# Two layers on graphs: the first pairs of phase A start closer together, and a broadcast add becomes a bias

## The chip, the cores and the metric

The kernel runs on one core of a Trainium2 chip. The metric is the device time of one execution in microseconds; of several executions the median counts. The core has five engines with a queue each: TensorE (PE in the profile) for matrix products, VectorE (DVE), ScalarE (ACT) and GpSimd (POOL) for elementwise work, and SyncE (SP), which here issues all DMAs. They run side by side and wait for each other by semaphores. Each works off its own queue in order.

## The reference

128 graphs of 64 nodes with 768 features, all in float32. Layer 0 is a graph attention with 12 heads of 64, followed by a gate, a residual and a layer norm. Layer 1 is a masked attention with 6 heads of 128, followed by the same.

```python
# layer 0
h = einsum('bnd,ade->bane', x, W);  th = tanh(h)
attn = einsum(th, w_src) + swapaxes(einsum(th, w_dst), 2, 3)   # src of the row + dst of the column
attn = where(attn >= 0, attn, 0.2 * attn)
attn = softmax(where(~adj[:, None], -999.0, attn))
f = elu(einsum('banm,bame->bane', attn, h) + b)
gate = sigmoid(x @ H_w.T + H_b)
x = layernorm(x + gate * f + (1 - gate) * x)
# layer 1
q, k, v = x @ Wq + bq, x @ Wk + bk, x @ Wv + bv
probs = softmax(q k^T / sqrt(128) + where(adj, 0, -9e15))
x = layernorm(x + (probs v) @ Wf + bf)
```

## The kernel before

The 8192 rows (graph, node) are 64 tiles of 128 rows, that is, two graphs each. Two tiles make a pair; there are NP = 32 pairs. Phase A does layer 0 and the v of layer 1, pair by pair. Phase B does the rest of layer 1 and isn't touched.

**Products.** A pair's dense product (W for h, G for the gate, V for layer 1's v) is done in the manner of Strassen, by seven blocks instead of eight. `Product.matmuls` (L217) issues block i as three matmuls of 128 x 384 (L208), which stand in the trace as six. Blocks 0, 2, 4 and 6 add into one PSUM bank X; block 1 has Z, blocks 3 and 5 have Y. Between them the partial sums must be taken out: after blocks 0, 2 and 3 ScalarE copies the bank to a `snap` (L404), after blocks 1, 4 and 5 VectorE adds bank and snap into the result (L427, L446), and after block 6 ScalarE copies it (L425, L444). So block 2 waits for the snap of block 0, block 4 for that of block 2, and block 5 for that of block 3. The left operands are the transposed rows T and four sums S of them, made by GpSimd (`token_sums`, L254).

**Transposed rows.** VectorE turns blocks of 32 x 32 (`turn`, L383), and the DMAs `load_blocks` (L370, four issues a tile) set the blocks into place. Layer 1's v needs the output of layer 0 in this form: it is spilled to DRAM (`spill`, L621), loaded as blocks (`x1_in`), turned and stored (`x1T`), and summed (`x1_sums`).

**Steps.** The order is written out by hand. `at(step, f)` puts a function on a list, and `run` (L262) calls the lists step by step; what is called emits instructions in that order, for each engine's queue. Within a step the order is that of the calls of `at`: earlier pairs come first. A step is one block of a dense product. Pair p starts at o = N * p with N = 21: W in steps o to o+6, G in o+7 to o+13, and in o+14 to o+20 the V of the pair two before it (v = o + 56, L736). Three pairs are moved by hand: V of pair NP-4 (28) goes to the end (o + 84), with its T loaded again from DRAM (`reload_T`); NP-2 and NP-1 have 50 and 45. So steps 14 to 20 of pairs 0, 1 and NP-2 (30) hold no V.

**The chain of a tile.** The rest of a pair is a chain for each tile, `Tile0`; tile 1 starts at s = o, tile 0 at s = o + 5 (L678). With s as zero: tanh of h on ScalarE (6; tile 0 one later), products with w_dst and w_src on GpSimd (7, 8), their sums on VectorE (9, 10), `dst_out` to DRAM and `exchange` of half of h between partitions by DMA (9), `dst_in` back as a broadcast over the rows (12 or 13), `add` (17): GpSimd adds `src` as a broadcast (L515), ScalarE applies the leaky activation (Prelu, L518); `mask` and `top` on VectorE (18), `exp` head by head on ScalarE (19, 20; L531), `scale` on GpSimd (21, 22; L541), `probs` and `aggregate` on TensorE (24, 25; L552, L570), `elu`, `mix1`, `mix2`, `norm1`, `norm2`, `spill` (26 to 31). Where `z` is three less (tile 1 of pairs 0, 1 and NP-2) add, mask, exp and scale come three steps earlier. `gate_in` (GpSimd, L580) and `gate` (ScalarE, L584) come at o+14 to o+18.

**Places.** `xb` has seven places of a tile. x and the adjacency of a pair are loaded together at o - 20 (`load`, L319) into place (2p + i) % 7. h and the gate (`gt`) have three buffers each, T four, S two, s two, hx two. The blocks of x are asked for at o - 20 and o - 16 and turned at o - 6 and o - 5, earlier by `lead` in pairs 1, 2 and NP-1.

Of the kernel before, what the change touches and what calls it, by code (L numbers as in the profile page):

```python
# [61 lines left out]
def kernel(  # L62
# [31 lines left out]
    nc = tc.nc  # L94
    NB, S, D = x.shape
    A, _, E = W.shape
    HEADS = 6
    DH = D // HEADS
    NC = D // P
# [3 lines left out]
    NP = NT // 2  # L103
# [201 lines left out]
    def phase_a(ctx):  # L305
# [6 lines left out]
        st = [dict() for _ in range(NP)]  # L312
        sds = []
        for i in range(2):
            sd = k1.tile([P, 32], F32, name=f"sd{i}")
            nc.vector.memset(sd, 0.0)
            sds.append(sd)

        def load(p):  # L319
            d = st[p]  # L320
            d["x"] = []
            for i in range(2):
                t = xb[:, (2 * p + i) % 7]
                nc.sync.dma_start(t, x_t[2 * p + i])
                d["x"].append(t)
            d["adj"] = small.tile([P, 2, S], U8, name="adj")
            nc.sync.dma_start(d["adj"], adj_p[p])

        load(0)

        w0 = weight_tile(0)
        w0_v = w0.rearrange("p s c o -> p s (c o)").rearrange(
# [10 lines left out]

        def load_hrow(oc):

            name = ("gt", "gt", "gt", "z", "tmp", "th")[oc]
            hrows[oc] = k3.tile([P, D], F32, name=name, bufs=3 if oc < 3 else 1)
            nc.sync.dma_start(hrows[oc], H_w[oc * P : (oc + 1) * P, :])

        def hw_blocks(oc):  # L350
# [56 lines left out]
        def sums(d):  # L407
            Ss = k6.tile([P, 4, CH, P], F32, name="S")
            token_sums(Ss, *d["T"])
            d["S"] = Ss  # L410
# [44 lines left out]
        class Tile0:  # L455
# [55 lines left out]
                        d["cap"], d["adj"], BIG, L0_FILL, op0=ALU.mult, op1=ALU.add  # L511
                    )

            def add(self):
                nc.gpsimd.tensor_tensor(  # L515
                    self.s, self.s, self.src[:, :, None].to_broadcast([P, A, S]), ALU.add
                )
                nc.scalar.activation(self.s, self.s, AF.Prelu, alpha=LEAKY_ALPHA)  # L518

            def mask(self):  # L520
                c = self.d["cap"][:, self.i, None, :].to_broadcast([P, A, S])
# [105 lines left out]
        def at(step, *fs):  # L627
            events.setdefault(max(step, 0), []).extend(fs)
# [17 lines left out]

        at(9, lambda: nc.vector.tensor_scalar_add(b_bc, b_bc, 1.0))

        N = 21
        for p in range(NP):  # L650
            d, o = st[p], N * p
            d["p"] = p
            if p:
                at(max(o - 20, 1), lambda p=p: load(p))

            def xb_in(d, i):
                d.setdefault("xp", []).append(blocks(x_t[2 * d["p"] + i]))

            def xT(d, i):
                d.setdefault("T", []).append(turn(d["xp"][i]))  # L660

            if p:
                at(o - 20, lambda d=d: xb_in(d, 0))
                at(o - 16, lambda d=d: xb_in(d, 1))

                lead = {1: 7, 2: 5, NP - 1: 4}.get(p, 0)
                at(o - 6 - lead, lambda d=d: xT(d, 0))
                at(o - 5 - lead, lambda d=d: xT(d, 1))
                at(o - 4, lambda d=d: sums(d))
            else:  # L670
                at(0, lambda d=d: d.update(T=[transposed(t) for t in d["x"]]))
                at(0, lambda d=d: sums(d))
            at(o, lambda d=d: start_h(d))
            at(o + 7, lambda d=d: start_g(d))
            for i in range(7):
                at(o + i, lambda d=d, i=i: dense(d, "W", i))
                at(o + 7 + i, lambda d=d, i=i: dense(d, "G", i))
            for i, s in ((1, o), (0, o + 5)):  # L678
                t = Tile0(p, i)
                at(s + 6 + (i == 0), t.tanh, t.cap)  # L680
                at(s + 7, t.dst_mul)
# [9 lines left out]
                at(z + 18, t.mask, t.top)  # L691
                at(z + 19, lambda t=t: t.exp(0))

                at(z + (19 if i else 20), lambda t=t: t.exp(1))
                at(z + 21, lambda t=t: t.scale(0))
                at(z + 22, lambda t=t: t.scale(1))
# [16 lines left out]
            if p < NP - 1:  # L713
                at(o + 37, lambda d=d: x1_in(d, 1))
                at(o + 40, lambda d=d: x1_in(d, 0))
                at(o + 43, lambda d=d: x1T(d, 1, turn(d["xp", 1])))
                at(o + 46, lambda d=d: x1T(d, 0, turn(d["xp", 0])))
            else:
                for i in range(2):
                    at(o + 43 - i, lambda d=d, i=i: x1T(d, i, transposed(d["x"][i])))  # L720

            def reload_T(d):
                d["T"] = []
                for i in range(2):
                    t = k3.tile([P, NC, P], F32, name="T", bufs=4)
                    nc.sync.dma_start(t, xT_d[d["p"]][:, i])
                    d["T"].append(t)

            def x1_sums(d):
                d["T"] = [d["x1T", i] for i in range(2)]  # L730
                sums(d)

            if p != NP - 4:
                at(o + (47 if p < NP - 1 else 44), lambda d=d: x1_sums(d))

            v = o + {NP - 4: 84, NP - 2: 50, NP - 1: 45}.get(p, 56)  # L736
            if p == NP - 4:
                at(v - 7, lambda d=d: reload_T(d))
                at(v - 3, lambda d=d: sums(d))
# [5 lines left out]
            at(4 + c, lambda c=c: weight_sums(lambda s: w1[:, s, c], nc.vector))  # L745


        o = N * (NP - 1)
        early = []

        def load_early(i, src, k):
# [11 lines left out]
        run(events, N * NP + 60)  # L763
        return early


# [421 lines left out]
```

## Time and profile before

| | |
|---|---|
| time, median of 9 runs | 2934.31 us (2930.59 to 2937.62) |
| the profiled execution's own time | 2932.93 us |
| its span, first to last instruction | 2931.2 us |
| mean granted clock of TensorE | 0.991 |
| PE, weight load, DVE, ACT, POOL busy | 97%, 70%, 62%, 37%, 56% |
| DMA | 309.15 MB, 105 GB/s on the mean |

The span is cut into 40 slices of 73 us in the page's rows of digits. Phase A takes the first 21 of them, to about 1520 us. A line of a timeline has the start in us, the length, the engine, the line of the kernel, the operation, what it writes and reads, how many such instructions follow each other, and in brackets how long the engine idled before it and what ended that. A line of the waits has the sum in us, the number of times and the longest. A line of windows has the stretch, its length, then busy us and instructions of PE, weight load, DVE, ACT and POOL, the granted clock, and the DMA's share and GB/s.

### The profile page before, as it was taken

To read this page: it belongs to the slowest core of one execution; us is meant where nothing else is said; L and a number is where in the kernel's file an instruction comes from. 1 tells how busy PE (TensorE), PEld (TensorE's weight loads), DVE (VectorE), ACT (ScalarE), POOL (GpSimd) and SP (SyncE) were. 2 spreads that over 40 slices of the span, in tenths; PEclk is the share of its full clock that TensorE was granted. 3 is DMA by queue.
4 is the path that set the end of the run, shared out by engine and by line. 5 is a ranking of instruction groups with operands and counts; after the bars stand their busy time and mean duration, and the time that the engine had idled before them with its cause. 6 is when DMAs were issued, how large, how long until landed. Compare 5 with 4: busy or idle time off the path is not lost.

```text
span 2931.2 us, 50050 instructions
## 1 busy us (share of the span) xinstructions
PE 2840.3 (97%) x18108; PEld 2063.8 (70%) x18108; DVE 1808.7 (62%) x3710; ACT 1074.3 (37%) x3035; POOL 1643.0 (56%) x1705
## 2 busy tenths in 40 slices
PE   7899999999999999999889999999999999999998
PEld 4455555555555555555458888888888888888887
DVE  4766767667677676676664555555555555555556
ACT  3455554554545545555432112222212222211223
POOL 3766566666665666665663544554554455454455
PEclk9999999999999999999999999999999999999999
DMA  6354453444544534435451122122112222212222
GB/s 185 85 149 127 131 149 113 133 147 111 148 125 133 149 112 133 146 112 149 127 192 34 54 67 88 55 88 88 69 62 77 65 78 87 79 56 74 88 82 71
DMA packets 358967, 309.15 MB, mean 105 GB/s; under 512 B 226624, under 2 KB 304192, under 8 KB 358720
## 3 DMA queue, kind: packets, MB, share of 16 engines
q1 hardware_dynamic: 358720, 305.95, 34.4%
q8 instruction: 144, 2.36, 0.3%
q14 instruction: 103, 0.84, 0.1%
HBM read 192.19 MB, written 101.06 MB: 100 GB/s over the span
## 4 chain that ended last, share of the span: by engine, by line
PE 57%; DVE 14%; POOL 12%; ACT 8%; DMA 5%; issue 3%; SPq 1%; POOLq 0%; DVEq 0%
PE X L854 41%; PE X L208 10%; ACT s L531 5%; POOL gt L580 3%; DMA xT_d<-T 2%; DVE s L522 2%; POOL th L475 2%; PE pb L994 2%; POOL s L541 2%; DVE nmx L526 2%; PE pb L919 2%; DVE pt L611 1%; POOL s L515 1%; DMA s<-dst_d 1%; DVE pt L602 1%
## 5 line engine op out<-in xcount | busy, mean ns | idle before, releaser
L208 PE MATMUL X<-w,S 128*128 128x384 f32 x2304 | 801.2, 493 | 48.8 <-ACT snap L404 45.5
L208 PEld LDWEIGHTS X<-w,S 128*128 128x128 f32 x2304 | 429.5, 191 | 346.2 <-issue 43.4
L854 PE MATMUL X<-S,w 128*128 128x256 f32 x2816 | 665.9, 382 | 3.7 <-DVE q L880 2.4
L208 PE MATMUL X<-w,T 128*128 128x384 f32 x1728 | 599.5, 490 | 1.6 <-DMA w<-in_L_gnn_W_dram 0.8
L854 PEld LDWEIGHTS X<-S,w 128*128 128x128 f32 x2816 | 525.4, 190 | 77.0 <-DVE q L880 2.8
L208 PEld LDWEIGHTS X<-w,T 128*128 128x128 f32 x1728 | 327.8, 191 | 224.7 <-issue 4.3
L836 POOL TENSOR_TENSOR Sc<-cT 128x256 f32<-128x256 f32 x224 | 161.3, 727 | 405.3 <-PE X L854 402.7
L854 PE MATMUL X<-w,Sc 128*128 128x256 f32 x1408 | 322.7, 381 | 1.9 <-POOL Sc L836 1.1
L897 DVE TENSOR_TENSOR xs<-xs,X 128x256 f32<-128x256 f32 x512 | 210.9, 420 | 170.9 <-PE X L854 161.3
L854 PEld LDWEIGHTS X<-w,Sc 128*128 128x128 f32 x1408 | 265.3, 190 | 40.3 <-POOL Sc L836 2.5
L531 ACT ACTIVATE s<-s,nmx 128x64 f32<-128x64 f32 x768 | 256.1, 335 | 94.1 <-DVE nmx L526 94.1
L880 DVE TENSOR_TENSOR k<-k,X 128x256 f32<-128x256 f32 x320 | 133.6, 421 | 218.0 <-PE X L854 168.1
L880 DVE TENSOR_TENSOR q<-q,X 128x256 f32<-128x256 f32 x320 | 133.2, 420 | 185.5 <-PE X L854 150.9
L541 POOL TENSOR_TENSOR s<-s,rs 128x384 f32<-128x384 f32 x128 | 128.2, 1003 | 209.6 <-DVE rs L539 140.5
L854 PE MATMUL X<-xb,w 128*128 128x256 f32 x960 | 236.6, 379 | 0.0
L404 ACT COPY snap<-X 128x384 f32<-128x384 f32 x288 | 136.1, 473 | 235.7 <-PE X L208 235.7
L302 ACT ACTIVATE xs<-xs,shift,rstd 128x768 f32<-128x768 f32 x62 | 63.5, 1025 | 419.9 <-POOL shift L298 411.7
L467 POOL TENSOR_TENSOR tmp<-th,wd_bc 128x768 f32<-128x768 f32 x64 | 138.7, 2167 | 132.2 <-ACT th L463 132.2
L875 ACT ACTIVATE k<-X,bk_c 128x256 f32<-128x256 f32 x192 | 90.9, 474 | 305.2 <-PE X L854 305.2
L854 PEld LDWEIGHTS X<-xb,w 128*128 128x128 f32 x960 | 181.2, 190 | 24.0
L875 ACT ACTIVATE q<-X,bq_c 128x256 f32<-128x256 f32 x192 | 90.9, 473 | 283.7 <-PE X L854 283.7
L968 POOL TENSOR_TENSOR s<-s,rs 128x384 f32<-128x384 f32 x60 | 49.7, 828 | 234.2 <-DVE rs L967 211.4
(111 smaller groups left out, 4110.5 us busy)
## 6 DMA issues: line engine op xcount, KB each, us to landing
xb<-in_x_dram SPq DMA_DIRECT2D x64, 384.0 KB
s<-dst_d SPq DMA_DIRECT2D x128, 192.0 KB
x_d<-xb SPq DMA_DIRECT2D x64, 384.0 KB
xT_d<-T SPq DMA_DIRECT2D x64, 384.0 KB
v_d<-v SPq DMA_DIRECT2D x128, 192.0 KB
xb<-xT_d SPq DMA_DIRECT2D x32, 768.0 KB
xb<-v_d SPq DMA_DIRECT2D x256, 96.0 KB
xs<-x_d SPq DMA_DIRECT2D x64, 384.0 KB
```

Source lines behind the costliest of these rows:

```text
L208: nc.tensor.matmul(o, self.lhsT(i, c), rhs, start=first and c == 0, stop=last and c == CH - 1, skip_group_check=True,)
L302: nc.scalar.activation(r, r, AF.Identity, bias=shift, scale=rstd)
L404: nc.scalar.copy(t, ps)
L467: nc.gpsimd.tensor_tensor(self.tmp, self.th, wd_bc, ALU.mult)
L531: nc.scalar.activation(self.s[:, a], self.s[:, a], AF.Exp, bias=self.nmx[:, a : a + 1], accum_out=self.sm[:, a : a + 1],)
L541: nc.gpsimd.tensor_tensor(t, t, rs[:, :, None].to_broadcast([P, A // 2, S]), ALU.mult)
L580: nc.gpsimd.tensor_tensor(self.g, self.g, hb_bc, ALU.add)
L836: nc.gpsimd.tensor_tensor(t, pair_part(d, q, r0), pair_part(d, q, r1), op)
L854: nc.tensor.matmul(ps, self.lhsT(r, slot, c), self.rhs(r, slot, c), start=start and c == 0, stop=stop and c == 1, skip_group_check=True,)
L875: nc.scalar.activation(o[:, b], ps, AF.Identity, bias=bias[:, hd : hd + 1], scale=1.0 if positive else -1.0)
L880: nc.vector.tensor_tensor(o[:, b], o[:, b], ps, ALU.add if positive else ALU.subtract)
L897: nc.vector.tensor_tensor(o, o, ps, ALU.add if positive else ALU.subtract)
```

## The change

Phase A's order is changed, and one operation of its chain. Line numbers in this section are those of the kernel before.

- Pairs 0 to 3 start at 0, 14, 28 and 42, all later ones at 21p - 21. V of pair p comes in steps 14 to 20 of pair p + 3; at the end V of NP-3 and NP-2 follow at 21 and 28 after the last pair's start, and NP-1 at 45 as before. `reload_T`, `lead` and `z` go.
- h has five fixed places (two in `xb`, three in `hp`), the gate four (one in `xb`, three in `gp`), x the remaining four of `xb`. x is loaded at o + 8, apart from the adjacency, which stays at o - 20.
- `exchange` moves from s + 9 to s + 16.
- GpSimd's add is left out. Instead ScalarE runs the leaky activation for each of the 12 heads with src as its bias: tile 1 in two halves at s + 15 and s + 16, tile 0 all at s + 17. `gate` of tile 1 moves from 16 to 17. The sums of Wv's blocks on GpSimd start at step 30 instead of 33.

```diff
+        h_at = [xb[:, 2], xb[:, 3], hp[:, 0], hp[:, 1], hp[:, 2]]
+        g_at = [xb[:, 4], gp[:, 0], gp[:, 1], gp[:, 2]]
...
-                t = xb[:, (2 * p + i) % 7]
+                t = xb[:, (0, 1, 5, 6)[(2 * p + i) % 4]]
...
-            d["h"] = [k3.tile([P, D], F32, name="h", bufs=3) for _ in range(2)]
+            d["h"] = [h_at[(2 * d["p"] + i) % 5] for i in range(2)]
...
-            d["g"] = [k3.tile([P, D], F32, name="gt", bufs=3) for _ in range(2)]
+            d["g"] = [g_at[(2 * d["p"] + i) % 4] for i in range(2)]
...
-            def add(self):
-                nc.gpsimd.tensor_tensor(
-                    self.s, self.s, self.src[:, :, None].to_broadcast([P, A, S]), ALU.add
-                )
-                nc.scalar.activation(self.s, self.s, AF.Prelu, alpha=LEAKY_ALPHA)
+            def add(self, part):
+                for a in range(part * A // 2, (part + 1) * A // 2):
+                    nc.scalar.activation(
+                        self.s[:, a], self.s[:, a], AF.Prelu, bias=self.src[:, a : a + 1],
+                        alpha=LEAKY_ALPHA,
+                    )
...
-                    33 + 8 * c + 2 * k,
+                    30 + 8 * c + 2 * k,
...
-        N = 21
+        O = [14 * p if p < 3 else 21 * p - 21 for p in range(NP)]
         for p in range(NP):
-            d, o = st[p], N * p
+            d, o = st[p], O[p]
             if p:
-                at(max(o - 20, 1), lambda p=p: load(p))
+                at(max(o - 20, 1), lambda p=p: load_adj(p))
+                at(o + 8, lambda p=p: load(p))
...
-                at(o - 20, lambda d=d: xb_in(d, 0))
-                at(o - 16, lambda d=d: xb_in(d, 1))
-                lead = {1: 7, 2: 5, NP - 1: 4}.get(p, 0)
-                at(o - 6 - lead, lambda d=d: xT(d, 0))
-                at(o - 5 - lead, lambda d=d: xT(d, 1))
+                at(max(o - 20, 1), lambda d=d: xb_in(d, 0))
+                at(max(o - 16, 1), lambda d=d: xb_in(d, 1))
+                at(o - 6, lambda d=d: xT(d, 0))
+                at(o - 5, lambda d=d: xT(d, 1))
...
-                at(s + 9, t.dst_sum, t.dst_out, t.exchange)
+                at(s + 9, t.dst_sum, t.dst_out)
                 at(s + 10, t.src_sum)
-                z = s - 3 if i and (p < 2 or p == NP - 2) else s
-                at(s + 12 if z < s else s + 13, t.dst_in)
-                at(z + 17, t.add)
+                at(s + 13, t.dst_in)
+                at(s + 16, t.exchange)
+                at(s + (15 if i else 17), lambda t=t: t.add(0))
+                at(s + (16 if i else 17), lambda t=t: t.add(1))
                 at(o + (14 if i else 16), t.gate_in)
-                at(o + (16 if i else 18), t.gate)
+                at(o + (17 if i else 18), t.gate)
...
-            v = o + {NP - 4: 84, NP - 2: 50, NP - 1: 45}.get(p, 56)
+            if p < NP - 3:
+                v = O[p + 3] + 14
+                times = ((1, v - 19, v - 13), (0, v - 16, v - 10))
+            elif p < NP - 1:
+                v = O[-1] + (21 if p == NP - 3 else 28)
+                times = ((1, v - 16, v - 7), (0, v - 15, v - 6)) if p == NP - 3 else (
+                    (1, v - 12, v - 7), (0, v - 10, v - 6)
+                )
+            if p < NP - 1:
+                for i, t0, t1 in times:
+                    at(t0, lambda d=d, i=i: x1_in(d, i))
+                    at(t1, lambda d=d, i=i: x1T(d, i, turn(d["xp", i])))
+                at(times[1][2] + 1, lambda d=d: x1_sums(d))
```

More of the change, by code (lines that the diff above doesn't have):

```diff
@@ L317, in phase_a, with load_adj @@
             sds.append(sd)
+        hp = k3.tile([P, 3, D], F32, name="hp")
+        gp = k3.tile([P, 3, D], F32, name="gp")
+        h_at = [xb[:, 2], xb[:, 3], hp[:, 0], hp[:, 1], hp[:, 2]]
+        g_at = [xb[:, 4], gp[:, 0], gp[:, 1], gp[:, 2]]
+        def load_adj(p):
+            t = small.tile([P, 2, S], U8, name="adj")
+            nc.sync.dma_start(t, adj_p[p])
+            st[p]["adj"] = t
         def load(p):
-            d = st[p]
-            d["x"] = []
+            st[p]["x"] = []
             for i in range(2):
-                t = xb[:, (2 * p + i) % 7]
+                t = xb[:, (0, 1, 5, 6)[(2 * p + i) % 4]]
                 nc.sync.dma_start(t, x_t[2 * p + i])
-                d["x"].append(t)
-            d["adj"] = small.tile([P, 2, S], U8, name="adj")
-            nc.sync.dma_start(d["adj"], adj_p[p])
+                st[p]["x"].append(t)
         load(0)
+        load_adj(0)
         w0 = weight_tile(0)
@@ L344, in load_hrow @@
         def load_hrow(oc):
-            name = ("gt", "gt", "gt", "z", "tmp", "th")[oc]
-            hrows[oc] = k3.tile([P, D], F32, name=name, bufs=3 if oc < 3 else 1)
+            if oc < 3:
+                hrows[oc] = gp[:, oc]
+            else:
+                hrows[oc] = k3.tile([P, D], F32, name=("z", "tmp", "th")[oc - 3])
             nc.sync.dma_start(hrows[oc], H_w[oc * P : (oc + 1) * P, :])
@@ L682, in phase_a @@
                 at(s + 8, t.src_mul)
-                at(s + 9, t.dst_sum, t.dst_out, t.exchange)
+                at(s + 9, t.dst_sum, t.dst_out)
                 at(s + 10, t.src_sum)
-                z = s - 3 if i and (p < 2 or p == NP - 2) else s
-                at(s + 12 if z < s else s + 13, t.dst_in)
-                at(z + 17, t.add)
+                at(s + 13, t.dst_in)
+                at(s + 16, t.exchange)
+                at(s + (15 if i else 17), lambda t=t: t.add(0))
+                at(s + (16 if i else 17), lambda t=t: t.add(1))
                 at(o + (14 if i else 16), t.gate_in)
-                at(o + (16 if i else 18), t.gate)
[L691 to L696, printed above, removed]
+                at(o + (17 if i else 18), t.gate)
+                at(s + 18, t.mask, t.top)
+                at(s + 19, lambda t=t: t.exp(0))
+                at(s + (19 if i else 20), lambda t=t: t.exp(1))
+                at(s + 21, lambda t=t: t.scale(0))
+                at(s + 22, lambda t=t: t.scale(1))
                 at(s + 24, t.probs)
@@ L711, in x1T @@
                 nc.sync.dma_start(xT_d[d["p"]][:, i], t)
[L713 to L727, printed above, removed]
             def x1_sums(d):
@@ L731, in x1_sums @@
                 sums(d)
-            if p != NP - 4:
-                at(o + (47 if p < NP - 1 else 44), lambda d=d: x1_sums(d))
-            v = o + {NP - 4: 84, NP - 2: 50, NP - 1: 45}.get(p, 56)
-            if p == NP - 4:
-                at(v - 7, lambda d=d: reload_T(d))
-                at(v - 3, lambda d=d: sums(d))
+            if p < NP - 3:
[11 more added lines that the diff above has]
+                at(times[1][2] + 1, lambda d=d: x1_sums(d))
+            else:
+                v = o + 45
+                for i in range(2):
+                    at(o + 43 - i, lambda d=d, i=i: x1T(d, i, transposed(d["x"][i])))
+                at(o + 44, lambda d=d: x1_sums(d))
             at(v, lambda d=d: start_v(d))
@@ L745, in phase_a @@
             at(4 + c, lambda c=c: weight_sums(lambda s: w1[:, s, c], nc.vector))
-        o = N * (NP - 1)
+        o = O[-1]
         early = []
@@ L762, in phase_a @@
         at(o + 30, lambda: load_T4(0))
-        run(events, N * NP + 60)
+        run(events, O[-1] + 80)
         return early
```

## The prediction, made before the changed kernel was run

> **What bounds the kernel now.** I read the page first, then who waited for whom on TensorE, then the timelines around the longest waits. The page says that TensorE (PE) is the wall: it is busy for 97% of the span, and its row is 9 except at the start, in two slices in the middle and in the last.
>
> ```profile
> PE 2840.3 (97%) x18108; PEld 2063.8 (70%) x18108; DVE 1808.7 (62%) x3710; ACT 1074.3 (37%) x3035; POOL 1643.0 (56%) x1705
> ...
> PE   7899999999999999999889999999999999999998
> ```
>
> So only its idle time, some 91 us, can be won by an edit that leaves the matmuls alone. The waits of PE (us in total, times, longest) say who holds it:
>
> ```profile
> PE X L208 <- ACT snap L404: 46.1, 34, 12.2
> PE pa L552 <- POOL s L541: 12.9, 33, 2.9
> ```
>
> The same view for 200 to 1390 us, 27 regular pairs of phase A:
>
> ```profile
> PE X L208 <- ACT snap L404: 8.7, 27, 0.3
> PE pa L552 <- POOL s L541: 7.7, 26, 0.3
> ```
>
> Regular pairs wait 0.3 us twice each. Nearly all the rest of the first line, some 37 us, lies outside. PE's timeline (start, length, what, idle before) shows three places:
>
> ```profile
> 47.84 4.03 PE L208 MATMUL X<-w,T 128*128 128x384 f32 x12
> 62.61 4.18 PE L208 MATMUL X<-w,S 128*128 128x384 f32 x6 [10.73 <-ACT snap L404]
> 66.58 1.38 PE L552 MATMUL pa<-ident,s 128*128 128x128 f32 x6
> 67.79 2.10 PE L208 MATMUL X<-w,S 128*128 128x384 f32 x6
> ...
> 108.42 3.98 PE L208 MATMUL X<-w,S 128*128 128x384 f32 x6 [12.03 <-ACT snap L404]
> ...
> 1420.33 4.18 PE L208 MATMUL X<-w,S 128*128 128x384 f32 x6 [12.24 <-ACT snap L404]
> ```
>
> These are pairs 1, 2 and the last (NP-1): each follows a pair whose steps 14 to 20 hold no V product. PE runs blocks 0 and 1 of the next W and stops before block 2, which adds into the bank that the snap must first copy out. ScalarE's (ACT) timeline shows why the snap is late:
>
> ```profile
> 53.72 0.84 ACT L518 ACTIVATE s<-s 128x768 f32<-128x768 f32 x1 [5.20 <-POOL s L515]
> ...
> 61.27 0.83 ACT L584 ACTIVATE gt<-gt 128x768 f32<-128x768 f32 x1
> 62.01 0.46 ACT L404 COPY snap<-X 128x384 f32<-128x384 f32 x1
> ```
>
> It stands behind the leaky activation, twelve exps and a gate of the pair before. The softmax chain needs its time, and PE has nothing to run in the empty slot.
>
> **What the Trainium skill says.** "ScalarE: Activation LUTs", section "What ACT_TABLE_LOAD costs": an ACTIVATE takes 186 ns + 0.833 ns a column, 93 ns more for each pointer operand, and neighbours overlap by about 93 ns. For 64 columns and one pointer operand that is an estimate of 332 ns, 240 ns apart. The trace agrees where such calls follow each other without accumulators:
>
> ```profile
> 2875.66 1.54 ACT L952 ACTIVATE s<-s,rs 128x64 f32<-128x64 f32 x6 [2.12 <-DVE rs L950]
> ```
>
> (1.54 - 0.332) / 5 = 0.242 us apart. "TensorE: Matmul & The Clock Gate", section "What's actually happening": after an idle window of about 3.4 us the array runs at half clock until it has been busy again. The trace agrees: the six matmuls after each long wait take about 4 us, and 2.1 elsewhere. "SBUF — State Buffer", section "SBUF: two separate sides": VectorE with two SBUF inputs and GpSimd exclude each other for an instruction's length. The trace fits: mask L522 takes 0.96 us, or 1.49 where it meets L259.
>
> **Change 1: the empty slots.** Pairs 0 to 2 begin 14 steps apart and every V lags three pairs, so no pair has an empty slot any more. Removed: waits of 10.73 + 12.03 + 12.24 = 35.0 us. The slow clock behind them goes too. From the first block's start to the next entry is 66.58 - 62.61 = 3.97 us, against 2.01 at a regular pair (699.76 to 701.77); the transposes after it take 1.21 instead of 0.65. That makes 2.5 us; the second place gives 1.8, the third 2.6: together 6.9. Three small waits of the same pairs (0.57, 1.30 and 0.86 us at 120, 116 and 158) go into the new order: 2.7. Sum: **-44.6 us**. As a check, three slots of seven steps of 1.934 us (727.0 to 730.86 is two) are 40.6 us, about what the stalls and the slow clock cost (41.9).
>
> **What the denser pairs cost.** A regular pair lasts 45.13 us (695.40 to 740.53). Its load comes from this window:
>
> ```profile
> 200.00:1390.00 1190.00, 1173.58 (x6183) 697.83 (x6183) 832.74 (x1371) 621.90 (x1973) 746.08 (x681) 1.00 0.46 133
> ```
>
> VectorE (DVE) has 832.74 / 1190 = 70%, 31.6 us a pair. Without a V (3 sums 0.47 apart) and the x1 transposes (4, 0.61 apart) 27.8 us are left, in 14 steps and two aggregations on PE: 14 x 1.934 + 3.2 = 30.3 us. That is 92%. ACT: 23.6 - 1.5 (V) + 4.3 (change 2) = 26.4 us, 87%. It fits, barely, so queues form.
>
> Where: (a) steps 15 to 18. The DMA of pair 2's blocks (step 8, four issues, 2.6 us) now stands ahead of pair 0's dst_out on SP, and four more (step 12) ahead of its dst_in. The two exchange issues (1.4 us) leave. Before, dst_in was issued at 46.53 and its reader ran at 52.22, 5.7 us later. Now: DVE frees the buffer at 41.5, blocks to 44.1, dst_out to 45.7, a weight block to 46.4, blocks to 49.5, dst_in at 49.5, landed at 55.2. Twelve leaky activations to 58.2, the snap behind them to 58.6. PE, started at 47.84, wants it before step 18: 47.84 + 4 x 1.934 = 55.6. A wait of **3 us** (bounds 0, if it lands as before, and 5). (b) steps 29 to 32: pair 0's mix1, mix2, dst_sum and norm1 put 7.8 us on DVE in three steps of 5.8; norm2 stands on ACT between the two halves of the leaky activation, and the snap of block 2 behind: **2 us** (0 to 5). (c) the same at step 43, with pair 2's x load behind the spill on SP ahead of dst_out: **3 us** (0 to 8). Sum **+8** (0 to 18). The five places of h and four of g cost no time: a place is written again only after its last reader (h of pair p's tile 0 is read at step 30, its place written at 32).
>
> **Change 2, in all 32 pairs.** GpSimd (POOL) loses 64 adds of 1.47 us, ACT 64 activations 0.75 apart, and gets 768 of 0.24: 2.9 us a tile instead of 0.75. For tile 1 (steps 15, 16) ACT has room: it idles 2.47 and 0.77 us at 733 to 735, and mask still waits for VectorE's V sum at 736.94, which PE sets. For tile 0 all twelve run in step 1, behind them the snap of block 2, two copies for the aggregation and six exps. Before: snap of block 0 at 699.14, a wait for POOL until 701.47, Prelu to 702.2, copies to 703.44, aggregation at 704.35. Now the activations start at 699.5 and end at 702.4, 0.2 later; the copies keep 0.7 us. The exps and the snap of block 3 (706.33 to 706.79) also move 0.2 to 0.3 us, and PE wants that snap at 707.35: slack 0.56 becomes about 0.3. So nothing, or little. The wait for dst_in moves from POOL's queue to ACT's, with the snaps and thus PE behind it. Tile 0's dst_in is issued at 737.94 and now wanted at 744.6, 6.7 us later; the one above took 5.7. The two 0.3 us waits stay: exp starts behind mask and maximum, and L541's second half behind VectorE's reciprocal. Bounds: -0.3 us a pair (one wait goes) to +0.6; I take +0.1, so 28 x 0.1 = **+2.8 us** (-8 to +17).
>
> **Moved, at no cost.** x is wanted at step 27 and now asked for at step 8, ahead of dst_out on SP, which waits there for DVE up to 9.7 us; without that idle it would cost its two issues, 1 us. The exchange (step 16) is wanted at step 25. Wv's sums start three steps earlier, still before the first V. Pair NP-4's reload of T (two DMAs) goes. The tail has three V products after the last pair's slot, as before, with the last lag changed: 0, bounds -3 and +3.
>
> **Sum.** -44.6 + 8 + 2.8 = -33.8. The profiled execution took 2932.93 us (span 2931.2), so 2899.1; the median of the nine runs lies 1.4 higher: **2900.5 us**. About 0.2% (6 us) is what a measurement here can tell from no change.
>
> **Rivals.**
> - A, the forecast: 0.68.
> - B, the gain is given back in the dense pairs: DVE at 92% and a two-engine chain lose the upper bound, 18 us, and more at a third junction, 25 in all: -44.6 + 25 + 2.8 = -16.8, 2917.5. For it: the load; against: regular pairs show no DVE wait on PE at 70%. 0.15.
> - C, regular pairs gain: without POOL's add the 0.3 us wait for L541 goes: -8 instead of +2.8, and junctions cost 3: -49.6, 2884.7. For it: 2.9 us less on POOL a pair; against: L541 waits for VectorE. 0.07.
> - D, slower: the burst in step 1. The slack is 0.3 us over 12 calls, so from 0.242 + 0.025 = 0.267 us a call PE waits; at about 0.37 the gain is gone; at 0.42 each pair waits 12 x 0.178 - 0.3 = 1.84 us, 28 x 1.84 = 51.5, in place of the 2.8: -44.6 + 8 + 51.5 = +14.9, 2949.2. For it: no Prelu of 64 columns is in the trace. Against: Prelu of 768 columns takes 844 ns, the same as tanh (847). 0.07.
> - E, the change does not do what it says: the long waits mostly move (B's 25 us) and change 2 costs its upper bound, 28 x 0.6 = 16.8: -44.6 + 41.8 = -2.8, 2931.5. 0.03.
>
> Low end: C, and A with junctions of 0 and the tail at -3: 2884. High end: B with the tail at +3, 2920. Faster is A, B and C (0.90), same E (0.03), slower D (0.07).
>
> **What would show it.** Right: no wait of over 4 us for a snap in pairs 1, 2 and the last; clock full from 25 us on; pairs 45.1 us apart; the leaky activations 0.24 us apart. Wrong: pairs over 45.5 us apart with PE waiting for the snaps (D), or waits on PE of over 10 us in total between 50 and 150 us (B).

## The result and the profile after

The changed kernel takes **2916.02 us** (median of 9 runs, 2913.76 to 2918.16) against 2934.22 of the kernel before (29 runs): a ratio of 0.994, with a 95% interval of 0.9932 to 0.9948. It is faster by 18.2 us. The forecast was 2900.5, a gain of 33.8; the time lies inside the range, and nearly on rival B's 2917.5. The profiled execution took 2917.93 us, its span 2916.2.

The lines that answer to those shown of before are, first, the page's share of PE and its 40 slices:

```profile
PE 2841.1 (97%) x18108; PEld 2063.6 (71%) x18108; DVE 1819.3 (62%) x3710; ACT 1203.0 (41%) x3739; POOL 1552.5 (53%) x1641
...
PE   8899999999999999999989999999999999999998
```

PE's work is the same; its idle time fell from 91 to 75 us. POOL lost 90 us, ACT gained 129. Who held PE, over the whole span (us in total, times, longest):

```profile
PE pa L566 <- POOL s L555: 17.5, 34, 3.4
PE X L209 <- ACT snap L416: 17.0, 35, 2.1
...
PE X L209 <- POOL s L555: 4.7, 1, 4.7
```

And from 200 to 1390 us:

```profile
PE X L209 <- ACT snap L416: 10.9, 26, 0.5
PE pa L566 <- POOL s L555: 8.4, 27, 0.3
```

The long waits for a snap have all but gone: 46.1 us became 17.0, and the longest that the view puts down to a snap is 2.1 instead of 12.2. But the waits for POOL's scale (L555) rose from 12.9 to 17.5, and they rose where the pairs are dense. PE's timeline there (start, length, what, idle before):

```profile
60.29 2.20 PE L209 MATMUL X<-w,S 128*128 128x384 f32 x6 [2.07 <-ACT snap L416]
...
86.28 0.55 PE L566 MATMUL pa<-ident,s 128*128 128x128 f32 x3 [2.40 <-POOL s L555]
86.67 3.39 PE L209 MATMUL X<-w,T 128*128 128x384 f32 x6
...
126.67 0.90 PE L566 MATMUL pa<-ident,s 128*128 128x128 f32 x3 [3.43 <-POOL s L555]
...
142.49 2.20 PE L209 MATMUL X<-w,S 128*128 128x384 f32 x6 [2.13 <-DVE hp L439]
...
186.89 3.57 PE L209 MATMUL X<-w,S 128*128 128x384 f32 x6 [4.70 <-POOL s L555]
```

In place of two waits of 10.7 and 12.0 us there are many of 0.2 to 4.7. The last line also shows the slow clock: six matmuls in 3.57 us instead of 2.2. It came after the wait of 2.40 us too (3.39), which is shorter than the idle window of some 3.4 us in the prediction, but not after those of 2.07 and 2.13. The wait of 4.70 in the last line is put down to POOL's scale, which ended last, at 186.88. But this block (block 2 of pair 4's W) reads no scaled scores; it adds into the bank that the snap of block 0 must first copy out, and that snap ended at 186.75, behind twelve exps and the second half of a norm:

```profile
184.11 0.33 ACT L545 ACTIVATE s<-s,nmx 128x64 f32<-128x64 f32 x1
...
185.36 1.03 ACT L303 ACTIVATE xb<-xb,shift,rstd 128x768 f32<-128x768 f32 x1 [0.46 <-POOL shift L299]
186.29 0.46 ACT L416 COPY snap<-X 128x384 f32<-128x384 f32 x1
```

So one wait of the old kind is left, at a place that the prediction does not name.

Where the gain is, is read from the starts of the products in PE's timeline. "Start section" is from the first block of pair 0's G to the first of pair 5's W. These two blocks, in the kernel before and then in the changed one:

```profile
32.49 4.03 PE L208 MATMUL X<-w,T 128*128 128x384 f32 x12
...
244.00 4.03 PE L208 MATMUL X<-w,T 128*128 128x384 f32 x12
```

```profile
34.96 4.03 PE L209 MATMUL X<-w,T 128*128 128x384 f32 x12
...
229.09 4.03 PE L209 MATMUL X<-w,T 128*128 128x384 f32 x12
```

Before, one V more has been done by then (seven blocks of 1.934 us, 13.54), and is taken off: 211.51 - 13.54. Between the Ws of pairs 5 and 31 it is added, since the pair with the empty slot lies there. Of the 44.6 us that the forecast removes, 29.8 lie in the start section and 14.8 (12.2 + 2.6) at the last pair.

| us | before | after | difference | predicted |
|---|---|---|---|---|
| from the span's start to pair 0's G | 32.49 | 34.96 | +2.5 | 0 |
| start section | 197.97 | 194.13 | -3.8 | -29.8 + 8 = -21.8 |
| W of pair 5 to W of pair 31 | 1173.60 | 1176.41 | +2.8 | 26 x 0.1 = +2.6 |
| W of pair 31 to the end of phase A's products | 119.13 | 103.26 | -15.9 | -12.2 - 2.6 = -14.8 |
| rest of the execution | | | -0.6 | 0 |

The sum is -15.0, the difference of the two profiled executions; the medians differ by 18.2, as one lies above and the other below its median. The first row is the wait for the first weights; it varied between 32.3 and 36.3 us over all runs of this case, whatever the kernel, so it is not the change's. The regular pairs, the last section and the rest came out near the forecast. **The start section is where the expected gain went**: the waits of 29.8 us left it, and 26.0 came back, not 8.

### The profile page after: what moved, and what is told of

The parts are those of the page before. It is cut to its first block, busy times and chain, and to the rows that moved or that the text cites. A ratio compares the mean times of both kernels' runs of the same rounds, so it can differ in the third digit from the quotient of the medians.

```text
span 2916.2 us, 50727 instructions
## 1 busy us (share of the span) xinstructions
PE 2841.1 (97%) x18108; PEld 2063.6 (71%) x18108; DVE 1819.3 (62%) x3710; ACT 1203.0 (41%) x3739; POOL 1552.5 (53%) x1641
## 4 chain that ended last, share of the span: by engine, by line
PE 73%; ACT 10%; DVE 9%; POOL 3%; issue 2%; DMA 1%; SPq 1%; DVEq 0%; ACTq 0%; POOLq 0%
PE X L866 42%; PE X L209 25%; ACT s L545 4%; PE pb L1006 2%; ACT s L529 2%; DVE s L536 2%; POOL s L555 2%; PE pa L584 2%; PE pb L931 2%; ACT snap L416 1%; PE pa L566 1%; DVE pt L617 1%; DVE pt L616 1%; ACT pt L612 1%; DVE nmx L540 1%
## 5 line engine op out<-in xcount | busy, mean ns | idle before, releaser
L555 POOL TENSOR_TENSOR s<-s,rs 128x384 f32<-128x384 f32 x128 | 128.2, 1002 | 222.6 <-DVE rs L553 120.7
L479 POOL TENSOR_TENSOR tmp<-th,wd_bc 128x768 f32<-128x768 f32 x64 | 137.6, 2150 | 123.5 <-ACT th L475 123.5
L529 ACT ACTIVATE s<-s,src 128x64 f32<-128x64 f32 x768 | 193.4, 338 | 5.7 <-DMA s<-dst_d 5.7
```

Of the source, the lines that this page charges most:

```text
L479: nc.gpsimd.tensor_tensor(self.tmp, self.th, wd_bc, ALU.mult)
L529: nc.scalar.activation(self.s[:, a], self.s[:, a], AF.Prelu, bias=self.src[:, a : a + 1], alpha=LEAKY_ALPHA,)
L555: nc.gpsimd.tensor_tensor(t, t, rs[:, :, None].to_broadcast([P, A // 2, S]), ALU.mult)
```

## The experiments

All are measured against the kernel before, and "start section" is that of the table, from one profiled execution. The kernel before was timed again beside each series: its medians were 2933.12 us beside experiments 1 to 4, 2933.35 beside 5 to 8 and 2932.06 beside 9 to 11, against 2934.22 beside the changed kernel. So where two medians of different series differ by some 3 us only, the medians alone do not show it, and the start section stands beside them.

**1. Change 2 alone, in the old order of the pairs.**

```diff
-                at(z + 17, t.add)
+                at(s + 15 if i and z == s else z + 17, lambda t=t: t.add(0))
+                at(s + 16 if i and z == s else z + 17, lambda t=t: t.add(1))
```

(with the new `add` of the changed kernel)

> The kernel before with the second part of the change alone: leaky activation head by head with src as bias (tile 1 at s + 15 and s + 16, tile 0 at s + 17, tile 1 of the three pairs with z = s - 3 all at z + 17), GpSimd's add gone; the steps stay 21 apart. Theory (the loss lies in the dense pairs, because VectorE's operations with two inputs and GpSimd's exclude each other there): regular pairs cost 0.1 us each, so 2937, between 2934 and 2941, and the three long waits for the snap stay. Rival (the bursts on ScalarE cost the time): they stand in all 32 pairs, so at least 5 us more than before, 2940 or more.

Measured: 2933.33 us, ratio 1.0003 (0.9994 to 1.0011). Pairs 6 to 29 begin 45.235 us apart instead of 45.138, so the price of +0.1 a pair is right; the start section is 2.3 us shorter, and the two cancel. The time lies just under the theory's 2934 to 2941 and well under the rival's 2940. Change 2 alone gives nothing that can be measured, and the three long waits stay (11.4, 10.7 and 12.6 us).

**2. Change 1 alone: the new order with GpSimd's add and one activation.**

```diff
-                at(s + (15 if i else 17), lambda t=t: t.add(0))
-                at(s + (16 if i else 17), lambda t=t: t.add(1))
+                at(s + 17, t.add)
```

(with the old `add`)

> The changed kernel with GpSimd's add and the one Prelu of 768 columns back at s + 17: the new order alone. Theory (VectorE against GpSimd in the dense pairs): 1.47 us a tile come back to GpSimd, 2.9 a dense pair, so the waits at the start grow by 3 to 9 us, the regular pairs win 0.1 each: 2916 + 6 - 3 = 2919, between 2915 and 2924. Rival (the bursts of leaky activations in front of the snaps make the waits of the dense pairs): most of the 15 us at the start go, 2898 to 2905.

Measured: 2924.16 us, ratio 0.9968 (0.9956 to 0.9979), at the upper end of what the theory had and far from the rival. ScalarE's bursts of twelve are not what fills the dense pairs: without them the start section is longer, 200.75 us against 194.13. Pairs are 45.147 us apart, and the last pair's section is 3.5 us longer (so the new order alone wins 12.4 of the 15.9 us there). Change 2 is worth nothing in the old order and 8 us in the new. What it takes away there is 2.9 us of GpSimd's time a pair, so the suspicion moves to GpSimd.

**3. Less on GpSimd: no sums of Wv.** The 12 sums of Wv, spread over steps 30 to 52, are left out; three of Wv's blocks are set to zero at step 1 instead.

```diff
-            for k in range(4):
-                at(
-                    30 + 8 * c + 2 * k,
-                    lambda c=c, k=k: weight_sums(lambda s: w2[:, s, c], nc.gpsimd, [k]),
-                )
+            at(1, lambda c=c: [nc.gpsimd.memset(w2[:, s, c], 0.0) for s in (2, 3, 5)])
```

> The changed kernel without the twelve sums of Wv's blocks on GpSimd (three blocks are set to zero at the start instead, so v is not computed rightly). They stand in steps 30 to 52, in the dense pairs. Theory (VectorE against GpSimd): some 6 us less of GpSimd in each of two dense pairs, so the waits at the start shrink by 6 to 12 us: 2904 to 2910. Rivals (ScalarE's bursts, late DMAs, the order of GpSimd's queue): no change by more than 2 us, 2914 to 2918.

Measured: 2912.71 us, ratio 0.9932 (0.9917 to 0.9947): 3.3 us less than the changed kernel, outside both expectations; the start section is 190.05 us, 4.1 less. GpSimd's load takes part, but a small one.

**4. The second half of tile 0's scale one step earlier.** This was to take away the wait of a regular pair for POOL's scale.

```diff
-                at(s + 22, lambda t=t: t.scale(1))
+                at(s + (22 if i else 21), lambda t=t: t.scale(1))
```

> The changed kernel with the second half of tile 0's scale at s + 21 instead of s + 22: its reciprocal goes ahead of mix1 on VectorE and the product ahead of dst_mul on GpSimd. Theory: the 0.3 us wait of PE for the scale goes in all regular pairs, 27 x 0.3 = 8 us; in the dense pairs the load is the limit, so waits only move, 0 to 3 us: 2905 to 2908. Rival (the order of GpSimd's queue makes the waits in the dense pairs): the 12.6 us of waits for the scale there go too, so 2896 to 2901.

Measured: 2940.21 us, ratio 1.0022 (1.0013 to 1.0032), that is 24 us slower than the changed kernel; both theories were wrong. The wait for POOL went, and a longer one came, in 25 pairs of the stretch from 210 to 1360 us. First PE's wait, then the timelines of POOL, DVE and ACT in one of these pairs:

```profile
PE pa L584 <- ACT pt L571: 27.4, 25, 1.4
```

```profile
755.16 1.84 POOL L479 TENSOR_TENSOR tmp<-th,wd_bc 128x768 f32<-128x768 f32 x1 [1.77 <-ACT th L475]
```

```profile
755.26 2.57 DVE L625 SCALAR_TENSOR_TENSOR pt<-gp,pt 128x768 f32<-128x768 f32 x1
```

```profile
758.91 0.86 ACT L571 COPY pt<-pa 128x384 f32<-128x384 f32 x2 [2.63 <-DVE xb L626]
```

With the scale out of its way, GpSimd's product L479 starts 0.1 us before VectorE's L625, and L625 takes 2.57 us instead of the 0.96 of L626 behind it. L625 ends 0.83 us after L479. The buffer `pt` comes free that much later, ScalarE's copy waits 2.63 us for it, PE behind that: pairs begin 45.99 us apart instead of 45.24. That an operation of VectorE with **two inputs in SBUF** and an operation of GpSimd don't run side by side was the theory from experiment 1 on; this trace shows it at work, and that the one which comes first sets who pays.

**5. A chain or a load? The norm of the first pairs later.** In pairs 0 to 2 the second half of the norm and the spill come a step or two later, the loads of x of pairs 1 to 4 three steps later.

```diff
-                at(o + 8, lambda p=p: load(p))
+                at(o + (11 if p < 5 else 8), lambda p=p: load(p))
...
-                at(s + 30, t.norm2)
-                at(s + 31, t.spill)
+                late = (1 if i else 2) if p < 3 else 0
+                at(s + 30 + late, t.norm2)
+                at(s + 31 + late, t.spill)
```

> The changed kernel with the normalisation (norm2) of pairs 0 to 2 later: tile 1 one step, tile 0 two steps, spill with it, the x loads of pairs 1 to 4 at o + 11. On ScalarE it then stands behind the leaky activations of the next pair and the snap, no longer ahead of them. Theory (in the dense pairs all engines are links of one chain of about 41 us a pair, and norm2 with its way over GpSimd is two of them): 2 to 3 us less in each of three pairs, 2907 to 2911. Rival (the lock between VectorE and GpSimd is the limit, whatever the order): no change by more than 2 us, 2914 to 2918.

Measured: 2912.54 us, ratio 0.9927 (0.9913 to 0.9942), 3.5 us less, between the two expectations; the start section is 190.39 us, 3.7 less. `norm2` stands on ScalarE ahead of the snap, and this was one link, not the main one.

**6. First pairs 17 steps apart.** If the density is the cost, a looser start should gain.

```diff
-        O = [14 * p if p < 3 else 21 * p - 21 for p in range(NP)]
+        O = [17 * p if p < 3 else 21 * p + -12 for p in range(NP)]
```

> The changed kernel with the first pairs 17 steps apart instead of 14 (0, 17, 34, 51, then 21 p - 12). Theory (a chain of 41 us a pair holds the early pairs, and PE needs only 36 at this distance): the early pairs take the same time, 2912 to 2920. Rival (the waits come from the queues being too dense and go with the distance): the nine steps without a block cost 9 x 1.93 = 17 us and the 27 us of waits and slow clock mostly go, 2905 to 2910.

Measured: 2936.35 us, ratio 1.001 (1.0001 to 1.0018); 16 us above the higher of the two expectations. The long waits are back, but not behind exps. PE, ACT and POOL at the second of them:

```profile
100.28 5.88 PE L209 MATMUL X<-w,S 128*128 128x384 f32 x12 [10.87 <-ACT snap L416]
```

```profile
98.92 0.84 ACT L598 ACTIVATE gp<-gp 128x768 f32<-128x768 f32 x1 [7.71 <-POOL gp L594]
99.67 0.46 ACT L416 COPY snap<-X 128x384 f32<-128x384 f32 x1
```

```profile
95.42 1.71 POOL L261 TENSOR_TENSOR S<-T,S 128x384 f32<-128x384 f32 x1
97.09 1.80 POOL L594 TENSOR_TENSOR gp<-gp,hb_bc 128x768 f32<-128x768 f32 x1
```

The gate of a pair (step 17) now stands on ScalarE ahead of the next pair's first snap, and waits for GpSimd's add L594, which stands behind the next pair's four sums of T (step 13 of this pair). At 14 steps the gate comes three steps after that snap. Not all of this need be the queues' doing: at 17 steps, steps 14 to 16 of each of the first three pairs hold no product, and the rival's expectation priced these nine steps at 17 us. The start section grew by 22.2 us, to 216.33. On that count the other waits grew by some 5 us, where the rival had them mostly go. A distance is not a degree of density: it decides which operations of two pairs are neighbours in a queue.

**7. Two of the four sums of T later.** From pair 4 on, the third and fourth sum move from step -4 to step 0, behind the scale of the pair before.

```diff
-                at(o - 4, lambda d=d: sums(d))
+                at(o - 4, lambda d=d, p=p: sums(d, (0,) if p > 3 else (0, 1)))
+                if p > 3:
+                    at(o, lambda d=d: token_sums(d["S"], *d["T"], part=(1,)))
```

> The changed kernel with the third and fourth sum of T (pairs 4 and later) at step o instead of o - 4, behind the scale of the pair before. Then nothing of GpSimd runs when VectorE wants to start the mask of tile 1 in a regular pair. Theory (in regular pairs PE waits 0.42 us for the snap because the mask is held 0.57 us by a sum on GpSimd, up from 0.53 before the change): mask 0.96 us instead of 1.53, the wait goes, 26 x 0.42 = 11 us: 2905, between 2903 and 2908. Rival (the exps or the copy ahead of the snap set it, not the mask): 2914 to 2918.

Measured: **2897.11 us**, ratio 0.9876 (0.9861 to 0.9891), 19 us less than the changed kernel and 8 less than expected. Pairs are 44.670 us apart instead of 45.244; that makes 15.0 of the 19 us. In DVE's timeline, mask of tile 1 in the changed kernel, with POOL's sum that overlaps it, and then mask in this kernel:

```profile
723.67 1.53 DVE L536 TENSOR_TENSOR s<-s,cap 128x768 f32<-128x768 f32 x1
```

```profile
723.39 1.00 POOL L260 TENSOR_TENSOR S<-T 128x384 f32<-128x384 f32 x1
```

```profile
724.17 0.96 DVE L538 TENSOR_TENSOR s<-s,cap 128x768 f32<-128x768 f32 x1 [1.94 <-ACT s L531]
```

1.53 - 0.96 = 0.57, and 45.244 - 44.670 = 0.574: mask's whole delay had reached PE in every pair, through maximum, exps and snap. The 0.4 us wait for the snap is gone from the regular pairs (from the start of a W's block 0 to that of its block 2 it is 3.87 us on the mean instead of 4.45; the view counts the wait from the end of the record ahead, and so less of it). The 0.3 for POOL's scale stays.

**8. Experiments 5 and 7 together.**

> The two last edits together, the later norm2 of pairs 0 to 2 and the divided sums. They touch different pairs, so the gains add: 2916 - 7 - 11 = 2898, between 2894 and 2904, if both theories hold; the one that holds alone otherwise.

Measured: **2893.87 us**, ratio 0.9864 (0.985 to 0.9879). The gains of 3.5 and 18.9 add up, to 22.2. This version beats both kernels, by 40 and 22 us.

**9. The dense pairs without the shared access.** In pairs 0 to 2, mask, mix1 and mix2 become reductions of one tensor.

```diff
             def mask(self):
+                if self.p < 3:
+                    self.spare(self.s)
+                    return
...
+            def spare(self, t):
+                nc.vector.tensor_reduce(
+                    small.tile([P, A], F32, name="spare"), t, AX.X, ALU.max
+                )
```

(and two `spare` in the place of each of mix1 and mix2)

> The changed kernel, but in pairs 0 to 2 the five VectorE operations a tile that read two SBUF tensors (mask, two of mix1, two of mix2) are replaced by reductions of one tensor of the same size, some 0.95 us each; the mask and the mixing of those three pairs are left out, so their values are not the reference's. Nothing else moves. Theory, the shared access: the operations take 0.53 us more than alone in the dense pairs, 30 of them 16 us, and GpSimd waits as long; with that gone the three dense pairs come down by 10 to 18 us: 2898 to 2906. Rival, the plain queue order: the operations would be late anyway, behind their neighbours in the queues, and only 2 to 6 us go: 2910 to 2914.

Measured: **2898.89 us**, ratio 0.9887 (0.9872 to 0.9902): 17 us less than the changed kernel, as the theory of shared access had it and the rival had not. The start section falls from 194.13 to 177.00 us. Groups of DVE between 75 and 146 us (busy us, mean ns), in the changed kernel and then here:

```profile
L617 DVE SCALAR_TENSOR_TENSOR pt<-pt,xb 128x768 f32<-128x768 f32 x4 | 7.4, 1841 | 0.1
L616 DVE SCALAR_TENSOR_TENSOR pt<-pt,z 128x768 f32<-128x768 f32 x4 | 5.9, 1486 | 4.6 <-ACT pt L612 4.4
...
L536 DVE TENSOR_TENSOR s<-s,cap 128x768 f32<-128x768 f32 x3 | 5.3, 1760 | 1.1 <-ACT s L529 1.1
```

```profile
L542 DVE TENSOR_REDUCE spare<-pt 128x12 f32<-128x768 f32 x8 | 7.6, 949 | 6.4 <-ACT pt L620 6.2
```

The replacements take 949 ns, what the originals take when nobody is in their way; so what left is the waiting for each other, not work. GpSimd's operations became shorter too: the scale (0.83 us instead of a mean of 1.18), L479 (1.82 instead of 2.28). The same 71 us, by engine (us and number of instructions for PE, PEld, DVE, ACT, POOL; then granted clock, DMA share, GB/s), in the changed kernel and here:

```profile
75.00:146.00 71.00, 59.66 (x355) 34.30 (x346) 59.25 (x83) 43.48 (x161) 55.02 (x47) 0.93 0.42 112
```

```profile
75.00:146.00 71.00, 66.59 (x395) 38.24 (x394) 52.01 (x96) 53.00 (x195) 54.36 (x57) 1.00 0.47 130
```

DVE does 96 instructions instead of 83 in less busy time, POOL 57 instead of 47 in the same. PE is at 66.6 us at full clock, where it was 59.7 at 0.93. Up to 210 us PE's waits for snaps, for POOL and for evictions sum to 9.1 us instead of 20.5 (11.4 less), and the clock accounts for 71 x 0.07 + 64 x 0.03 = 6.9 more: 18.3, about the 17.1 that were won. Whether it is VectorE's delay or GpSimd's that reaches PE was not separated; the edit frees both.

**10. The dense pairs without GpSimd's sums of T.**

```diff
             if p:
...
-                at(o - 4, lambda d=d: sums(d))
+                if p > 3:
+                    at(o - 4, lambda d=d: sums(d))
```

(W and G of pairs 1 to 3 then multiply a half of T)

> The changed kernel without GpSimd's four sums of T ahead of W and G in pairs 1 to 3 (these pairs multiply a half of T in place of the sums, so their values are not the reference's). 12 operations of some 1.6 us leave GpSimd's queue between 30 and 150 us. Theory, GpSimd's queue is what the dense pairs wait for: the scale of tile 1 and the mean and spread of the norm stand behind these sums, and 8 to 15 us go: 2901 to 2908. Rival, GpSimd has room and the chain is held elsewhere, as the run without Wv's sums suggests with its 3 us: 2912 to 2916.

Measured: 2913.33 us, ratio 0.9935 (0.9919 to 0.9952), 2.7 us less, which these intervals don't tell from nothing; in the trace the start section is 192.40 us, 1.7 less. The rival is right. With 12 operations taken from GpSimd's queue little opens. Between 75 and 146 us mask and the second of mix1 are no shorter than in the changed kernel (1.76 and 1.84 us), so they meet other operations of GpSimd:

```profile
L620 DVE SCALAR_TENSOR_TENSOR pt<-pt,xb 128x768 f32<-128x768 f32 x4 | 8.2, 2042 | 0.1
L539 DVE TENSOR_TENSOR s<-s,cap 128x768 f32<-128x768 f32 x3 | 5.3, 1760 | 1.1 <-ACT s L532 1.1
```

**11. Experiment 8 with the two sums late in all pairs.**

```diff
-                at(o - 4, lambda d=d, p=p: sums(d, (0,) if p > 3 else (0, 1)))
-                if p > 3:
-                    at(o, lambda d=d: token_sums(d["S"], *d["T"], part=(1,)))
+                at(o - 4, lambda d=d: sums(d, (0,)))
+                at(o, lambda d=d: token_sums(d["S"], *d["T"], part=(1,)))
```

> The kernel with both late steps, in which the third and fourth sum of T now move from step -4 to step 0 in all pairs, not only from pair 4 on. Theory, GpSimd's queue is what the dense pairs wait for: the scale of tile 1 no longer stands behind four sums in pairs 1 to 3, and 3 to 8 us go against the same kernel with the move from pair 4 on (2893.9): 2886 to 2891. Rival: in the dense pairs the queue is as full at step 0 as at step -4, so the time stays: 2893 to 2896.

Measured: 2896.73 us, ratio 0.988 (0.9865 to 0.9894), no difference from experiment 8 that these intervals can tell. In the regular pairs the move was worth 0.57 us each; in the dense ones the moved sums seem to meet other work instead: mask takes a mean of 1.85 us there between 75 and 146 us, 1.27 in experiment 8 (three instructions each).

## Why the prediction was right, and what it missed

**Right: the stalls go.** The time is inside the stated range, but only because that range was drawn to take in B: the forecast's own terms, with the dense pairs at their bound of 18, end at 2934.3 - 44.6 + 18 + 2.8 = 2910.5. What held is the following. The step "Removed: waits of 10.73 + 12.03 + 12.24 = 35.0 us", with the slow clock behind them, held. At the third place, where no pairs are denser, 14.8 were forecast and 15.9 measured; the new order alone gives 12.4 of them (experiment 2).

**Right in size: change 2's price.** Forecast +0.1 us a pair; measured 45.244 - 45.138 = +0.106, and 0.097 alone in experiment 1. It was picked between bounds of -0.3 and +0.6, and it lies elsewhere than the text looked: in the wait for the snap of block 0 (8.7 us over 27 waits became 10.9 over 26, 0.32 and 0.42 each), not in the slack before the snap of block 3. So this close a hit is partly luck. The twelve activations take 2.97 us at their 0.242 us pitch:

```profile
56.90 2.97 ACT L529 ACTIVATE s<-s,src 128x64 f32<-128x64 f32 x12 [3.98 <-DMA s<-dst_d]
59.78 0.46 ACT L416 COPY snap<-X 128x384 f32<-128x384 f32 x1
```

(12 - 1) x 0.242 + 0.338 = 3.0. So rival D (0.267 us a call) was never near. It also said that the two small waits stay, and they do.

**Right: term (a).** The lines above are that junction: the wait for dst_in, the burst, the snap behind. PE waited 2.07 us there; forecast 3.

**Wrong in size: "It fits, barely, so queues form", "Sum +8 (0 to 18)".** The dense pairs cost 29.8 - 3.8 = 26.0 us, outside the bounds of 0 to 18. The step that failed is the load check: 92% for VectorE and 87% for ScalarE, each against PE's 30.3 us, GpSimd not counted at all. VectorE's 27.8 us were summed from durations of regular pairs, in which its two-input operations meet GpSimd less often. Mask and the first of mix1, in the kernel before, from 300 to 1280 us:

```profile
L522 DVE TENSOR_TENSOR s<-s,cap 128x768 f32<-128x768 f32 x43 | 53.0, 1233 | 44.8 <-DMA xT_d<-T 44.8
...
L602 DVE SCALAR_TENSOR_TENSOR pt<-pt,z 128x768 f32<-128x768 f32 x44 | 42.2, 958 | 16.7 <-ACT pt L598 13.7
```

With the pairs closer together there are more meetings, and the durations themselves grow: mask from 1.23 us to 1.76, the two of mix1 from 0.96 each to 1.49 and 1.84. A sum over both engines would have given warning; as an estimate from the durations of these traces it is 9.6 us of two-input operations of VectorE a pair (10 x 0.96), and some 20 us of GpSimd's (4 sums of T at 1.0, 4 products at 1.81, 4 scales at 0.83, 2 gate adds at 1.81, the norm's small ones 2 x 0.94), with Wv's sums some 6 more: 35.6 in 30.3 us of PE. In a regular pair it is 33.6 (with V's sums) in 45. But this sum does not price the loss: experiments 3 and 10 each took twelve operations out of it, some 12 us, and the start section fell by 4.1 and 1.7 us only. So which operations meet seems to count for more than how many there are.

What is left beside this is seen in experiment 9: without the shared access of pairs 0 to 2 the dense pairs cost 29.8 - (197.97 - 177.00) = 8.8 us. So 17.1 of the 26.0 go with the shared access. That the 8.8 come so near to the +8 of the text is luck in part. PE then waits 1.8 us at junction (a), forecast 3; not at all in steps 29 to 32, where (b) had 2; 1.0 each at steps 42 and 46, about (c), which had 3; and 2.8 at block 2 of pair 4's W (step 65), for which the text has no term.

The prediction had named the means. From the Trainium skill, "SBUF — State Buffer", section "SBUF: two separate sides", was cited with mask at 1.49 us, and then used in no term of the sum. Its section "Who interferes with whom" adds that the order of issue decides who waits, and that a reduction doesn't contend: experiment 4 shows the first (2.57 us against 0.96), experiment 9 the second (949 ns). The Trainium skill's "Perfetto Trace Analysis", section "Identifying the Most-Contended Engine", calls occupancy a fair measure of how near VectorE and GpSimd are to their limit. Here it misleads, since a record's length takes in the time for which it is held up: between 75 and 146 us VectorE is busy for 59.25 of 71 us with 83 instructions, and for 52.01 with 96 in experiment 9.

**The rivals.** B's time was right, and its words half: it blamed VectorE's 92% and a third junction, and its sign, over 10 us of waits between 50 and 150 us, came (13.9 us). A third junction did come, at step 65. Of the signs of being right, the full clock from 25 us on did not come: it was 0.93 between 75 and 146 us. C did not come: the 0.3 us wait for POOL's scale stays, as "against" had it. E had the first half nearly right, as 26.0 us came back against its 25, and was wrong about change 2.

**Open.** Change 2 gains 8 us in the new order (experiments 1 and 2). That its add on GpSimd, gone, meets fewer masks and mixes fits experiment 9, but was not shown; nor was what holds PE at step 65 taken apart. Separate buffers for the transposed probabilities and elu's exp, which share `pt`, were not tried.

## What to carry to other kernels

Before you make pairs or tiles denser, look at what shares an access, not only at what shares an engine: VectorE's operations with two inputs in SBUF and GpSimd's operations hold each other up, and a duration from a stage in which they seldom meet is too short for one in which they do. Their sum against the bounding engine's time warns of it, but did not give the loss here. What the sharing costs can be measured by putting a reduction of one tensor, of the same size, in the place of the two-input operations (experiment 9). Look for the operation that is stretched and lies on the chain to the bounding engine (mask here, 0.57 us a pair), and move its neighbour on the other engine; that gave 19 us, as much as the whole change, 15 of them in the regular pairs. A new distance between overlapping pairs must be checked for which operations become neighbours in each queue: 17 steps instead of 14 brought back stalls of 11 us, though these also take in the three steps without a product.

## What was not expected of the hardware

That the two engines exclude each other stands in the prediction; by how much was not expected. An operation of VectorE with two inputs in SBUF took 0.96 us alone and up to 2.6 us beside GpSimd, where the prediction had 1.49. GpSimd's own took longer as well: a sum of Wv of 1.00 us took 1.71. From the changed kernel's dense pairs, POOL and DVE:

```profile
109.35 1.81 POOL L487 TENSOR_TENSOR th<-th,ws_bc 128x768 f32<-128x768 f32 x1
111.13 1.71 POOL L173 TENSOR_TENSOR w<-w 128x384 f32<-128x384 f32 x1
```

```profile
109.40 2.59 DVE L536 TENSOR_TENSOR s<-s,cap 128x768 f32<-128x768 f32 x1 [1.10 <-ACT s L529]
```

L487 starts 0.05 us ahead of mask and takes its usual 1.81; mask ends at 111.99, 0.83 after L487, so it did its 0.96 us of work almost wholly after it. The sum L173, whose record begins at 111.13, ends at 112.84, 0.85 after mask, of its 1.00. They took turns.
